# Two graph-attention layers on one core: where the store of the output stands in SyncE's order

## The chip, the core and the metric

The kernel runs on one core of a Trainium2 chip. A core has TensorE (PE in the profile, with its weight loads as PEld), VectorE (DVE), ScalarE (ACT), GpSimd (POOL) and SyncE (SP), which here does nothing but issue transfers. The metric is the time of one execution on the device in microseconds; lower is better.

## What is computed

The input is a batch of 64 graphs of 256 nodes with 512 features each, and an adjacency matrix for each graph. Two layers follow one another, each of the form x = x + layer(relu(layernorm(x))):

```python
# layer 0: two GAT sublayers, mask = adj or the diagonal, softmax over the sources
h = elu(gat_layer(h, mask, W1, att_src1, att_dst1, b1, concat=True))   # 4 heads of 256
h = gat_layer(h, mask, W2, att_src2, att_dst2, b2, concat=False)       # 1 head of 512
# layer 1: one sublayer, 8 heads of 64, mask = adj, softmax over the targets, relu
scores = leaky_relu(a_src[i] + a_dst[j] + b_att);  out = relu(softmax(scores) @ xh)
```

The graphs don't depend on each other.

## The kernel before

Each graph goes through three attention sublayers, numbered 1, 2 and 3 in the names of the steps. A sublayer is a product with the weights (`m1a` and `m1b`, `m2`, `m3`, each a set of seven smaller products, L54), the exponentials of the attention terms (`exp1`, `exp2`, `exp3`), the weights of the edges (`edges`, L280 on ScalarE and L281 on VectorE), a product with these (`gat1` L382, `gat2` L434, `gat3` L484), and a step that divides and adds on VectorE (`out1` L392, `out2` L444, `out3` L492). 128 nodes stand across the partitions, so a graph has two row tiles (T = 2).

**How a term gets to all partitions.** The edges need a term of every node along the free axis, alike on every partition. `spread` (L230) does it by way of DRAM: ScalarE issues a small write of the exponentials (`kept<-exs`, L233; 8 KB in `exp3`, 1 KB in `exp2`, 4 KB in `exp1`), and SyncE issues the reads that hand it to all 128 partitions (`bc<-kept`, L238; four of 256 KB in `exp3`, one of 128 KB in `exp2`, two of 256 KB in `exp1`). A read has to wait until the write has landed. L280 on ScalarE waits for the read.

**How the layernormed input is turned.** `away1` writes h to DRAM and reads it back in another layout (L200, L201); VectorE then transposes it (`back`, L206) for the products of `m1a` and `m1b`.

**The order.** There is no scheduler at work (`manual_schedule`): every engine runs its instructions in the order in which the program states them. A string named `order` is that order; it is gone through once for each round r from 1 to 63, with a `head` before and a `tail` after. An item such as `-2 store` is a step of graph r - 2, so that three or four graphs are under way in a round: graph r + 1 is loaded, normalised and multiplied by W1, graph r goes through sublayer 1 and into sublayer 2, graph r - 1 from sublayer 2 into 3, and graph r - 2 finishes sublayer 3. An item places its instructions on every engine that it uses, behind those of the items ahead of it; the place of `store`, which is one transfer on SyncE, matters on SyncE alone.

**SyncE in a round**, before: `cap3` (two transposing transfers, L363), `load` (xs and ad, L292 and L294), `away1` (L200, L201), the four reads of `exp3`, the read of `exp2`, the store of graph r - 2 (L501), the two reads of `exp1`. An instruction that waits holds up those behind it.

**The store.** `store` writes the tile x2 of graph r - 2, 512 KB, to the output. x2 is completed by four additions on GpSimd, two rows of tiles by two halves (`out3`, L494), the last of which is `-2 out3 1 0`. The pool of x2 has two buffers; `out2` of a later graph writes into the one that the store has freed.

Each transfer tells of its landing on one of eight semaphores that are given out in turn. [...]

Of the kernel before, what the change touches and what calls it, by code (L numbers as in the profile page):

```python
# [97 lines left out]
def short_path(ctx, tc, flags, x, adj, w1, att_src1, att_dst1, b1, w2, att_src2, att_dst2, b2, w_proj, w_att,  # L98
# [451 lines left out]
    class Weights:  # L550
# [66 lines left out]
        -2 edges3 7, -2 gat3 0 0, -2 edges3 5, -2 gat3 0 1, -1 edges2, 0 m1b p7, -2 out3 0 1, -2 out3 0 0,  # L617
        -1 gat2 0, 0 m1b c22, -1 out2 0, -1 stats3 0, 0 m1b p3, -1 gat2 1, 0 edges1 0, 0 edges1 1, 0 m1b p4,
        -1 out2 1, 0 cap3, 1 load, 0 gat1 0 0, 0 edges1 2, 0 edges1 3, 0 out1 0 0, -2 gat3 1 1, -2 gat3 1 0,
        -1 stats3 1, 0 gat1 0 1, -1 norm3, -2 out3 1 1, -2 out3 1 0, 0 out1 0 1, 0 elu1 0 0, 0 elu1 0 1, 0  # L620
        gat1 1 0, -1 turn3, 0 out1 1 0, 0 gat1 1 1, 0 out1 1 1, 1 stats1, -1 m3 p1, 0 turn2 0 0, 0 turn2 0
        1, 0 elu1 1 1, 0 elu1 1 0, -1 m3 p2, -1 m3 p5, 1 masks, 1 norm1, -1 m3 p6, 0 m2 p1, 0 turn2 1 0, 0
        turn2 1 1, 1 away1, -1 m3 p7, 1 bias, -1 m3 c22, 0 m2 p2, -1 m3 p4, -2 range, -1 m3 p3, -1 exp3, 1
        turn1, 0 m2 p6, 0 m2 p5, 0 m2 p7, 1 caps, 1 m1a p1, 0 m2 c22, 0 m2 p3, 0 m2 p4, 0 exp2, 1 m1a p6, -2
        store, -1 edges3 0, -1 edges3 1, 1 m1b p1, 1 m1a p7, 1 m1a p5, 1 m1a c22, -1 edges3 2, 1 m1a p2, -1
        edges3 4, 1 m1a p3, -1 edges3 3, 1 m1a p4, 1 m1b p2, 1 exp1, -1 edges3 6, 1 m1b p6, 1 m1b p5
    """
    tail = """
# [270 lines left out]
@with_exitstack  # L899
def gat_layers(ctx, tc, *args):  # L900
    nc = tc.nc
    pool = ctx.enter_context(tc.tile_pool(name="flags", bufs=1))
    flags = pool.tile([1, 1], I32, name="flags")
    short_path(tc, flags, *args)
    B = args[0].shape[0]
    count = nc.values_load(flags[0:1, 0:1], min_val=0, max_val=B)
    general_path(tc, count, *args)
# [24 lines left out]
```

## Time and profile before

| what | before |
|---|---|
| time, median of 3 runs | 3341.45 us (3340.55 to 3341.65) |
| span of the profiled execution | 3279.7 us |
| mean granted TensorE clock | 0.993 |
| TensorE busy | 3155.8 us, 96% |
| VectorE busy | 2267.6 us, 69% |
| ScalarE busy | 1959.6 us, 60% |
| GpSimd busy | 1178.3 us, 36% |
| transfers | 279.19 MB, 85 GB/s on average |

The busy times are those of an engine's own instructions; the issue of a transfer is not counted. The span of the profile runs from the first to the last instruction; the time of a run contains some 62 us more.

Three kinds of lines are used below. A line of the timeline has the start in us, the length in us, the engine (with a q where only its sequencer is at work), the line of the kernel, the operation, the tiles as out<-in, how many instructions are merged, and in brackets how long the engine stood idle before it and what ended that. A line of the waits says who waited for what, the total in us, how often, and the longest. A line of the table of stretches has the stretch, its length, for PE, PEld, DVE, ACT and POOL the busy time and the number of instructions, then the granted clock, the busy share of the 16 DMA engines and what they moved in GB/s. `kept<-exs`, `bc<-kept` and `out_dram<-x` are the small write, the read over all partitions and the store.

### The profile page before, as it was taken

How to read it: one execution, taken by the hardware profiler on the slowest of the kernel's cores; microseconds unless marked ns; L12 is line 12 of the kernel's file. 1: busy time of each engine (PE TensorE's matmuls, PEld its weight loads, DVE VectorE, ACT ScalarE, POOL GpSimd, SP SyncE). 2: the span in 40 equal slices, each digit the busy share in tenths (PEclk: the TensorE clock that was granted, in tenths of full speed). 3: DMA queues.
4: the chain of work that ended last, by engine and by line, in shares of the span. 5: the costliest groups of instructions: out<-in, count | busy, mean ns of one | idle time of the engine just before them, and what ended most of it. 6: DMA issues, size and time to landing. Idle time of an engine off the chain costs nothing. (4 is left out here: it accounts for less than half of the span.)

```text
span 3279.7 us, 60652 instructions
## 1 busy us (share of the span) xinstructions
PE 3155.8 (96%) x21808; PEld 2663.1 (81%) x21808; DVE 2267.6 (69%) x6189; ACT 1959.6 (60%) x4867; POOL 1178.3 (36%) x1433
## 2 busy tenths in 40 slices
PE   4999999999999999999999999999999999999997
PEld 3788888888888888888888888888888888888886
DVE  7667667667667677676676676676776766766765
ACT  2566566566556566655665565566566556665654
POOL 3243343343343342332433433423333334334332
PEclk8999999999999999999999999999999999999998
DMA  4222333323323333323223223233333233332231
GB/s 140 65 79 83 88 87 85 88 88 78 94 82 84 88 82 91 86 83 89 80 82 91 87 79 88 82 91 86 83 91 86 82 89 81 78 94 87 79 94 34
DMA packets 350751, 279.19 MB, mean 85 GB/s; under 512 B 157936, under 2 KB 252016, under 8 KB 350448
## 3 DMA queue, kind: packets, MB, share of 16 engines
q1 hardware_dynamic: 240688, 272.31, 28.3%
q10 hardware_dynamic: 109760, 2.95, 1.9%
q8 instruction: 177, 2.90, 0.4%
q14 instruction: 126, 1.03, 0.2%
HBM read 199.36 MB, written 67.43 MB: 81 GB/s over the span
## 5 line engine op out<-in xcount | busy, mean ns | idle before, releaser
L280 ACT ACTIVATE wy<-bc,exs 128x256 f32<-128x256 f32 x1646 | 746.9, 524 | 263.8 <-DMA bc<-kept 199.4
L281 DVE SCALAR_TENSOR_TENSOR e<-wy,exs,cap 128x256 f32<-128x256 f32 x1024 | 452.2, 483 | 223.0 <-ACT wy L280 223.0
L382 PE MATMUL pm<-xl,e 128*128 128x257 f32 x2048 | 500.3, 387 | 57.5 <-DVE e L281 21.7
L253 DVE TENSOR_TENSOR xl<-pm,kept 128x256 f32<-128x256 f32 (+2 forms) x768 | 321.8, 419 | 282.7 <-PE pm L54 196.9
L494 POOL TENSOR_TENSOR x<-x,o 128x256 f32<-128x256 f32 x256 | 181.0, 728 | 930.9 <-DVE r L490 884.2
L54 PE MATMUL sum<-w_sb,h1s 128*128 128x257 f32 x2048 | 489.0, 381 | 9.3 <-POOL h1s L213 7.0
L382 PEld LDWEIGHTS pm<-xl,e 128*128 128x128 f32 x2048 | 365.5, 190 | 151.4 <-DVE e L281 36.5
L60 ACT ACTIVATE kept<-sum 128x264 f32<-128x264 f32 (+3 forms) x768 | 276.7, 376 | 310.7 <-PE sum L54 294.3
L54 PEld LDWEIGHTS sum<-w_sb,h1s 128*128 128x128 f32 x2048 | 389.4, 190 | 68.7 <-POOL h1s L213 7.2
L54 PE MATMUL pm<-w_sb,h1s 128*128 128x257 f32 x1536 | 370.7, 383 | 10.4 <-DVE xl L253 7.1
L178 POOL TENSOR_TENSOR rstd<-ve,neg_half 128x2 f32<-128x2 f32 x128 | 117.6, 919 | 683.5 <-DVE ve L176 683.5
L54 PEld LDWEIGHTS pm<-w_sb,h1s 128*128 128x128 f32 x1536 | 286.7, 190 | 74.7 <-POOL hs L213 20.7
L281 DVE SCALAR_TENSOR_TENSOR e<-wy,exs,mask 128x256 f32<-128x256 f32 x640 | 276.0, 482 | 65.9 <-ACT wy L280 65.6
L484 PEld LDWEIGHTS pm<-xl,e 128*64 128x64 f32 x8192 | 251.8, 138 | 45.2 <-DVE e L281 23.3
L54 PE MATMUL sum<-w1a_sb,hs 128*128 128x260 f32 x1024 | 269.8, 386 | 11.7 <-DVE w1a_sb L520 4.1
L54 PE MATMUL sum<-w1b_sb,hs 128*128 128x256 f32 x1024 | 271.7, 388 | 4.1 <-ACT hs L343 1.9
L484 PE MATMUL pm<-xl,e 128*64 128x65 f32 x8192 | 270.4, 224 | 1.9 <-DVE e L281 1.2
L54 PE MATMUL sum<-wp_sb,hs 128*128 128x264 f32 x1024 | 271.0, 387 | 1.1 <-ACT kept L60 1.1
L395 ACT ACTIVATE ez<-z 128x512 f32<-128x512 f32 x256 | 159.8, 624 | 181.6 <-DVE z L392 181.6
L392 DVE SCALAR_TENSOR_TENSOR z<-pm,r,b_sb 128x256 f32<-128x256 f32 x512 | 247.8, 484 | 18.3
L434 PE MATMUL pm<-xl,e 128*128 128x257 f32 (+1 forms) x1024 | 243.8, 381 | 1.2 <-DVE e L281 1.2
L54 PEld LDWEIGHTS sum<-w1a_sb,hs 128*128 128x128 f32 x1024 | 190.7, 190 | 51.1 <-issue 13.2
(97 smaller groups left out, 4962.9 us busy)
## 6 DMA issues: line engine op xcount, KB each, us to landing
bc<-kept SPq DMA_DIRECT2D x380, 256.0 KB
xs<-in_x_dram SPq DMA_DIRECT2D x64, 512.0 KB
out_dram<-x SPq DMA_DIRECT2D x64, 512.0 KB
kept_h<-h SPq DMA_DIRECT2D x63, 512.0 KB
h<-kept_h SPq DMA_DIRECT2D x63, 512.0 KB
ad<-in_adj_dram SPq DMA_DIRECT2D x64, 256.0 KB
bc<-kept SPq DMA_DIRECT2D x63, 128.0 KB
w_sb<-in_L_gnn_W_dram SPq DMA_DIRECT2D x4, 512.0 KB
```

The source lines that it names most:

```text
L54: self.nc.tensor.matmul(to[:, :self.n], self.lhs[:, i, c, :], self.rhs[:, i, c, :], start=(first and c == 0), stop=(last and c == self.nk ...
L60: self.nc.scalar.activation(s[:, :self.n], self.sum[:, :self.n], AF.Copy)
L178: nc.gpsimd.tensor_tensor(rstd, ve[:, 0, :], neg_half, ALU.pow)
L253: nc.vector.tensor_tensor(dst, pm, add, ALU.add)
L280: nc.scalar.activation(wy, bc, AF.Copy, scale=yw)
L281: nc.vector.scalar_tensor_tensor(dst, wy.rearrange("p t q -> p (t q)"), xw, mask, ALU.max, op)
L382: nc.tensor.matmul(pm[:, :Q + 1], self.e[1, h][:, s, t * P:(t + 1) * P], xl1[:, s, h, L1:], start=(s == 0), stop=(s == T - 1))
L392: nc.vector.scalar_tensor_tensor(z[:, sl], pm[:, :Q], r, b1_sb[:, sl], ALU.mult, ALU.add)
L395: nc.scalar.activation(ez, z[:, 2 * g * F1:2 * (g + 1) * F1], AF.Relu, scale=-1.0)
L434: nc.tensor.matmul(pm[:, :n], self.e[2][:, s, t * P:(t + 1) * P], xl2[:, s, half, L2:L2 + n], start=(s == 0), stop=(s == T - 1))
L484: nc.tensor.matmul(pv[q:q + 64, h, :], self.e[3, a * G + h][:, s, t * P + q:t * P + q + 64], xl3[:, s, a * G + h, :], start=(s == 0), stop ...
L494: nc.gpsimd.tensor_tensor(to, to, o.rearrange("p h k -> p (h k)"), ALU.add)
```

## The change

The item `-2 store` goes from the end of the round, behind `1 m1a p6`, to right behind `-2 out3 1 0`, the last addition to its tile. It is meant to send the output off as soon as it is complete. In SyncE's order the store then stands behind `load` and ahead of `away1`; everything else keeps its order. The head and the tail, which has the last two stores, are as before.

```diff
-        -1 stats3 1, 0 gat1 0 1, -1 norm3, -2 out3 1 1, -2 out3 1 0, 0 out1 0 1, 0 elu1 0 0, 0 elu1 0 1, 0
+        -1 stats3 1, 0 gat1 0 1, -1 norm3, -2 out3 1 1, -2 out3 1 0, -2 store, 0 out1 0 1, 0 elu1 0 0, 0
...
-        turn1, 0 m2 p6, 0 m2 p5, 0 m2 p7, 1 caps, 1 m1a p1, 0 m2 c22, 0 m2 p3, 0 m2 p4, 0 exp2, 1 m1a p6, -2
-        store, -1 edges3 0, -1 edges3 1, 1 m1b p1, 1 m1a p7, 1 m1a p5, 1 m1a c22, -1 edges3 2, 1 m1a p2, -1
+        m1a p6, -1 edges3 0, -1 edges3 1, 1 m1b p1, 1 m1a p7, 1 m1a p5, 1 m1a c22, -1 edges3 2, 1 m1a p2, -1
```

The lines between are the same items, broken at other places.

More of the change, by code (lines that the diff above doesn't have):

```diff
@@ L619, in short_path @@
         -1 out2 1, 0 cap3, 1 load, 0 gat1 0 0, 0 edges1 2, 0 edges1 3, 0 out1 0 0, -2 gat3 1 1, -2 gat3 1 0,
-        -1 stats3 1, 0 gat1 0 1, -1 norm3, -2 out3 1 1, -2 out3 1 0, 0 out1 0 1, 0 elu1 0 0, 0 elu1 0 1, 0
-        gat1 1 0, -1 turn3, 0 out1 1 0, 0 gat1 1 1, 0 out1 1 1, 1 stats1, -1 m3 p1, 0 turn2 0 0, 0 turn2 0
-        1, 0 elu1 1 1, 0 elu1 1 0, -1 m3 p2, -1 m3 p5, 1 masks, 1 norm1, -1 m3 p6, 0 m2 p1, 0 turn2 1 0, 0
-        turn2 1 1, 1 away1, -1 m3 p7, 1 bias, -1 m3 c22, 0 m2 p2, -1 m3 p4, -2 range, -1 m3 p3, -1 exp3, 1
-        turn1, 0 m2 p6, 0 m2 p5, 0 m2 p7, 1 caps, 1 m1a p1, 0 m2 c22, 0 m2 p3, 0 m2 p4, 0 exp2, 1 m1a p6, -2
-        store, -1 edges3 0, -1 edges3 1, 1 m1b p1, 1 m1a p7, 1 m1a p5, 1 m1a c22, -1 edges3 2, 1 m1a p2, -1
+        -1 stats3 1, 0 gat1 0 1, -1 norm3, -2 out3 1 1, -2 out3 1 0, -2 store, 0 out1 0 1, 0 elu1 0 0, 0
+        elu1 0 1, 0 gat1 1 0, -1 turn3, 0 out1 1 0, 0 gat1 1 1, 0 out1 1 1, 1 stats1, -1 m3 p1, 0 turn2 0 0,
+        0 turn2 0 1, 0 elu1 1 1, 0 elu1 1 0, -1 m3 p2, -1 m3 p5, 1 masks, 1 norm1, -1 m3 p6, 0 m2 p1, 0
+        turn2 1 0, 0 turn2 1 1, 1 away1, -1 m3 p7, 1 bias, -1 m3 c22, 0 m2 p2, -1 m3 p4, -2 range, -1 m3 p3,
+        -1 exp3, 1 turn1, 0 m2 p6, 0 m2 p5, 0 m2 p7, 1 caps, 1 m1a p1, 0 m2 c22, 0 m2 p3, 0 m2 p4, 0 exp2, 1
+        m1a p6, -1 edges3 0, -1 edges3 1, 1 m1b p1, 1 m1a p7, 1 m1a p5, 1 m1a c22, -1 edges3 2, 1 m1a p2, -1
         edges3 4, 1 m1a p3, -1 edges3 3, 1 m1a p4, 1 m1b p2, 1 exp1, -1 edges3 6, 1 m1b p6, 1 m1b p5
```

## Prediction

> **What bounds the kernel now.** I read the page first, for the engine that is nearly full and how little of it is idle.
>
> ```profile
> span 3279.7 us, 60652 instructions
> PE 3155.8 (96%) x21808; PEld 2663.1 (81%) x21808; DVE 2267.6 (69%) x6189; ACT 1959.6 (60%) x4867; POOL 1178.3 (36%) x1433
> ```
>
> TensorE (PE) is the bound; a change that only moves a store can win no more than TensorE's idle time. The table of stretches says where that is. I cut the span at the first L434 matmul (`gat2`) of each round. The rows are one round without the store, three with it, and the 59 rounds from 201.25 to 3143.63 together; the second number is the round's length, the third TensorE's busy time.
>
> ```profile
> 152.44:201.25 48.81, 48.60 (x341) 41.49 (x340) 34.71 (x94) 30.62 (x76) 18.18 (x22) 1.00 0.32 88
> 1596.30:1647.17 50.87, 48.92 (x341) 41.24 (x340) 34.66 (x95) 30.53 (x76) 18.17 (x22) 1.00 0.30 84
> 1494.98:1545.98 51.00, 48.91 (x341) 41.27 (x340) 34.70 (x95) 30.55 (x76) 18.16 (x22) 1.00 0.34 83
> 2446.26:2494.91 48.65, 48.50 (x341) 41.49 (x340) 34.70 (x95) 30.52 (x76) 18.19 (x22) 1.00 0.29 87
> 201.25:3143.63 2942.38, 2882.47 (x20061) 2438.95 (x20060) 2048.34 (x5546) 1802.18 (x4484) 1072.12 (x1298) 1.00 0.31 86
> ```
>
> The same work takes 48.65 to 51.00 us at a clock of 1.00 throughout; the mean is 2942.38 / 59 = 49.87. So a round that waits for nothing takes about 48.7, and 1.2 us a round is lost. Third view, the waits of TensorE from 110 to 3160 us (total, times, longest):
>
> ```profile
> PE pm L382 <- DVE r L390: 21.1, 48, 0.6
> PE pm L382 <- DVE r L490: 13.2, 52, 0.3
> PE pm L382 <- DVE e L281: 12.1, 21, 1.2
> PE pm L54 <- DVE xl L253: 6.1, 40, 0.2
> ```
>
> 46 us of it stand before L382, `gat1`, in the first microseconds of a round: VectorE is late with `edges1` (L281), then with `out1` and `out3`, which stand behind them on VectorE. Why it is late shows in the timeline of one such round, ScalarE, SyncE and TensorE in turn:
>
> ```profile
> 1589.08 0.39 SPq L501 DMA_DIRECT2D out_dram<-x  x1
> 1591.35 0.37 ACTq L233 DMA_DIRECT2D kept<-exs  x1
> 1598.31 0.79 SPq L238 DMA_DIRECT2D bc<-kept  x2
> 1601.62 1.77 ACT L280 ACTIVATE wy<-bc,exs 128x256 f32<-128x256 f32 x4 [4.73 <-DMA bc<-kept]
> 1602.71 2.00 PE L382 MATMUL pm<-xl,e 128*128 128x257 f32 x8 [1.06 <-DVE e L281]
> ```
>
> and in the one full round that has no store to make (round 1: graph -1 doesn't exist):
>
> ```profile
> 147.49 0.37 ACTq L233 DMA_DIRECT2D kept<-exs  x1
> 150.63 0.79 SPq L238 DMA_DIRECT2D bc<-kept  x2
> 157.63 1.90 PE L382 MATMUL pm<-xl,e 128*128 128x257 f32 x8
> ```
>
> The chain is `exp1`'s 4 KB write of exs to DRAM (L233), its read back over all partitions (L238, issued only once the write has landed), then L280, L281, L382. From write to read it takes 1598.31 - 1591.35 = 6.96 us with the store issued 2.3 us ahead of the write, and 3.14 without; and there TensorE waits for nothing. I took these points in every round: with the store 4.2 to 7.0, median 5.7 (61 rounds); the three writes without it (two in the head, one in round 1) took 3.03, 4.62 and 3.14.
>
> **What the Trainium skill says.** "DMA: Bandwidth & Descriptors", section "Queues, rings and completion order": SyncE's and ScalarE's queues are rings on the same 16 engines, served in turn, and the write that raises a transfer's semaphore lands only after all earlier writes of that engine, across its queues. So the small write must wait out the store's writes even where its own bytes are through. The trace agrees: the last 8-byte packet of the write leaves a median 2.6 us after issue with the store and 1.7 in round 1, and from there the read follows after 3.1 and 1.4 us. Same page, "Latency and other measured facts": the receipt from HBM grows with load; here the whole write to read grows from 3.14 to 5.7.
> "Perfetto Trace Analysis", "Per-instruction lifecycle": a DMA's bar is its issue, not its movement. So I read movement from the DMA share of stretches, here 2 us each, then the stretch in which the store will stand:
>
> ```profile
> 147.50:149.50 2.00, 2.00 (x12) 1.49 (x10) 1.67 (x5) 1.80 (x7) 0.00 (x0) 1.00 0.64 61
> 1591.00:1593.00 2.00, 2.00 (x11) 1.75 (x10) 1.80 (x5) 1.80 (x8) 0.00 (x0) 1.00 0.97 242
> 1662.00:1671.00 9.00, 9.00 (x52) 7.86 (x51) 7.43 (x22) 7.15 (x13) 4.17 (x6) 1.00 0.00 0
> ```
>
> While the write goes out, the engines are 97% busy at 242 GB/s with the store, and 64% at 61 GB/s without.
>
> **The change, part by part.**
> *What moves.* No instruction is added or removed; 62 of the 64 stores (rounds 2 to 63) go up SyncE's order, from behind bc2's read to behind `load` and ahead of `away1`. On the other engines only names and the numbers of DMA semaphores shift.
> *What is taken away.* The store from ahead of `exp1`'s write. Then the read of bc1 is issued 1.1 us (5.7 to 4.6) to 2.6 us (5.7 to 3.1) earlier. What a round gains I take from the 59 rounds: with d the time from the L434 anchor to bc1's issue (mean +0.65 us), the length follows 48.75 + 0.97 x max(0, d + 0.50) us; by groups, d under -0.2 gives 48.73 (6 rounds), 0.2 to 0.7 gives 49.63 (13), over 1.3 gives 50.70 (8). So all of the lateness is paid, down to d = -0.5. Moving every d earlier by 1.0, 1.5 and 2.5 us gives mean lengths of 49.09, 48.85 and 48.75: 46, 60 and 66 us over 59 rounds. I take 1.5, between the ends, because three writes are few and an instruction fetch crosses them at times: 60 us. The tail's first round, with a late bc1 too (4.29 us of wait on ScalarE), may add 1; I leave it out.
> *What the store meets at its new place.* It waits for GpSimd's last addition. In the round at 1647 that ends at 1660.39 + 1.42 = 1661.81. Behind it on SyncE stands `away1`'s write, which waits for ScalarE's `norm1` until 1671.17: the store waits on 5 us in which SyncE would have waited anyway, and 9.4 us remain for 512 KB. Where it stands now its packets take 2.6 us (from 0.6 before the small write's issue to 2.0 after); with about 1 us to the first packet and 3 to the landing, an estimate from the small write's own 3.14, it is over by 1668. The DMA engines carry nothing from 1662 to 1671, and no tile for `turn2`, `m3` or `stats1` is in transfer then: cost nothing.
> *Buffers.* x2 (two buffers) comes free some 29 us sooner (1691.08 to about 1662); VectorE waited for that 0.3 us once in the whole run. Nothing.
> *Sum.* 3341.45 - 60 = 3281.
>
> **The rivals.**
> *Less of it:* the small write is slow for another reason as well. bc2's read, just ahead of it, and instruction fetches stay; the write in the head without a store took 4.62. A gain of only 0.5 us in d gives 49.44 a round: 26 us, 3316. Against it: the longest wait for bc1 and the store's last packet go together (0.82 between the last packets of store and write).
> *No change:* once bc1 comes in time, L382 waits for `out1` or `out3` through VectorE's own queue, so that the reciprocals' 34 us stay: 3341.45 - 12 at most for L281 alone, and with an unlucky rest 3338. Against it: round 1, and the fast rounds such as 2446.26, have none of these waits at equal VectorE work (34.7 us).
> *Slower:* the store collides with `away1`: write and read back of h (1671.17, 1674.42), which VectorE's L206 awaited in 58 rounds, 46 us in all, so the path has no slack. If it ran on 1 us into it, 62 x 1 would be lost against the 60 won; if 1.5 and half the gain comes, 3341 + 93 - 30 = 3404. Against it: the 9.4 us.
>
> **How the numbers follow.** Most of the gain, 3281: 0.67. Less of it, 3316: 0.20. No change: 0.06. Slower: 0.07. The lower end of the range is all lateness gone, 66 us and a little from head and tail: 3270. The upper end takes in the partial case: 3318. Faster by over 0.2% (below 3334.8) is the first two: 0.87; the same 0.06; slower 0.07.
>
> **What would show it.** In the profile after: from L233's 4 KB write to bc1's read about 3.1 to 4.2 us instead of 5.7; rounds of 48.7 to 48.9 us; TensorE's waits before L382 down from 46 us to under 10; the store issued some 13 to 14 us after the L434 anchor, and the DMA share between 1662 and 1671 of such a round no longer 0. TensorE's busy time stays near 3150. I am wrong if that write still takes over 5 us, if L382 still waits for VectorE in most rounds, or if L206's wait for h grows above its 46 us.

## The result, and the profile after

The changed kernel takes 3228.09 us (median of 4 runs, 3224.51 to 3231.37), against 3341.55 us before (3340.55 to 3341.86). The ratio is 0.9661, with a 95% interval of 0.9644 to 0.9677: faster by 113 us. The forecast was 3281 us with a range of 3270 to 3318, so the direction was right and the gain almost twice as large.

The head of the page after, to be read against the two lines of before:

```profile
span 3227.2 us, 60529 instructions
PE 3146.1 (97%) x21808; PEld 2670.1 (83%) x21808; DVE 2266.0 (70%) x6189; ACT 1963.0 (61%) x4867; POOL 1178.1 (37%) x1433
```

The busy times are nearly the same; the span is 52.5 us shorter. This is the first thing to notice: between the two traces lie 52.5 us, between the timed runs 113. The table of stretches, for the same 59 rounds and for one of them:

```profile
204.78:3092.43 2887.65, 2870.73 (x20062) 2444.60 (x20061) 2046.90 (x5547) 1805.56 (x4484) 1072.01 (x1298) 1.00 0.33 87
1624.82:1673.49 48.67, 48.52 (x341) 41.49 (x340) 34.73 (x95) 30.66 (x76) 18.19 (x22) 1.00 0.31 87
```

The mean round is 2887.65 / 59 = 48.94 us (median 48.81), where it was 49.87. TensorE's waits from 110 to 3100 us:

```profile
PE pm L54 <- DVE xl L253: 4.8, 32, 0.2
PE pm L382 <- DVE r L490: 2.3, 10, 0.3
PE pm L382 <- DVE r L390: 2.2, 6, 0.6
PE pm L434 <- DVE e L281: 2.0, 2, 1.2
PE sum L54 <- ACT kept L60: 1.9, 7, 0.4
PE pt L193 <- ACT h L186: 1.8, 2, 1.5
PE pm L382 <- DVE e L281: 1.4, 2, 0.7
```

What stood before L382 was 46.4 us (12.1 for L281, 34.3 for the two reciprocals); it is 5.9. Of the 54.7 us that the 59 rounds are shorter, that is some 40; another 11.7 is TensorE's busy time, 2870.73 instead of 2882.47 for the same matmuls, which the profile doesn't explain. The timeline of one round, ScalarE, SyncE and TensorE:

```profile
1619.87 0.37 ACTq L233 DMA_DIRECT2D kept<-exs  x1
1623.55 0.79 SPq L238 DMA_DIRECT2D bc<-kept  x2
1627.55 1.90 ACT L280 ACTIVATE wy<-bc,exs 128x256 f32<-128x256 f32 x4 [2.15 <-DMA bc<-kept]
1630.01 1.90 PE L382 MATMUL pm<-xl,e 128*128 128x257 f32 x8
1637.46 0.38 SPq L501 DMA_DIRECT2D out_dram<-x  x1
1646.80 0.37 SPq L200 DMA_DIRECT2D kept_h<-h  x1
```

From exp1's small write to the read of bc1 it takes 3.68 us here instead of 6.96, and L382 starts with no wait. The store is issued 12.6 us after the first L434 (at 1624.82) and 9.3 us ahead of `away1`. VectorE's wait for what `away1` reads back is about what it was (46.0 us before):

```profile
DVE hs L206 <- DMA h<-kept_h: 47.2, 56, 2.1
```

### The profile page after: what moved, and what is told of

Read it like the earlier page. It is cut to its first block, busy times and chain, and to the rows that moved or that the text cites. A ratio compares the mean times of both kernels' runs of the same rounds, so it can differ in the third digit from the quotient of the medians.

```text
span 3227.2 us, 60529 instructions
## 1 busy us (share of the span) xinstructions
PE 3146.1 (97%) x21808; PEld 2670.1 (83%) x21808; DVE 2266.0 (70%) x6189; ACT 1963.0 (61%) x4867; POOL 1178.1 (37%) x1433
## 5 line engine op out<-in xcount | busy, mean ns | idle before, releaser
L280 ACT ACTIVATE wy<-bc,exs 128x256 f32<-128x256 f32 x1646 | 745.4, 524 | 187.5 <-DMA bc<-kept 141.7
L281 DVE SCALAR_TENSOR_TENSOR e<-wy,exs,cap 128x256 f32<-128x256 f32 x1024 | 452.0, 483 | 223.4 <-ACT wy L280 223.3
L382 PE MATMUL pm<-xl,e 128*128 128x257 f32 x2048 | 495.6, 387 | 15.1 <-DVE e L281 10.2
L54 PE MATMUL sum<-w_sb,h1s 128*128 128x257 f32 x2048 | 489.1, 381 | 9.3 <-POOL h1s L213 7.0
L382 PEld LDWEIGHTS pm<-xl,e 128*128 128x128 f32 x2048 | 374.0, 190 | 87.6 <-issue 14.1
L54 PEld LDWEIGHTS sum<-w_sb,h1s 128*128 128x128 f32 x2048 | 389.4, 190 | 68.7 <-POOL h1s L213 7.2
L54 PE MATMUL pm<-w_sb,h1s 128*128 128x257 f32 x1536 | 371.2, 383 | 10.4 <-DVE xl L253 5.9
L54 PEld LDWEIGHTS pm<-w_sb,h1s 128*128 128x128 f32 x1536 | 287.0, 190 | 74.8 <-POOL hs L213 17.0
L281 DVE SCALAR_TENSOR_TENSOR e<-wy,exs,mask 128x256 f32<-128x256 f32 x640 | 276.1, 482 | 15.6 <-ACT wy L280 15.3
L54 PE MATMUL sum<-w1a_sb,hs 128*128 128x260 f32 x1024 | 270.2, 387 | 7.9 <-ACT kept L60 2.9
L54 PE MATMUL sum<-w1b_sb,hs 128*128 128x256 f32 x1024 | 272.6, 389 | 4.2 <-DVE w1b_sb L520 2.2
L54 PE MATMUL sum<-wp_sb,hs 128*128 128x264 f32 x1024 | 271.0, 387 | 1.1 <-ACT kept L60 1.1
L434 PE MATMUL pm<-xl,e 128*128 128x257 f32 (+1 forms) x1024 | 245.6, 382 | 3.5 <-DVE e L281 3.4
L54 PEld LDWEIGHTS sum<-w1a_sb,hs 128*128 128x128 f32 x1024 | 190.7, 190 | 47.7 <-issue 13.4
```

What stands on the lines that cost most here:

```text
L54: self.nc.tensor.matmul(to[:, :self.n], self.lhs[:, i, c, :], self.rhs[:, i, c, :], start=(first and c == 0), stop=(last and c == self.nk ...
L280: nc.scalar.activation(wy, bc, AF.Copy, scale=yw)
L281: nc.vector.scalar_tensor_tensor(dst, wy.rearrange("p t q -> p (t q)"), xw, mask, ALU.max, op)
L382: nc.tensor.matmul(pm[:, :Q + 1], self.e[1, h][:, s, t * P:(t + 1) * P], xl1[:, s, h, L1:], start=(s == 0), stop=(s == T - 1))
L434: nc.tensor.matmul(pm[:, :n], self.e[2][:, s, t * P:(t + 1) * P], xl2[:, s, half, L2:L2 + n], start=(s == 0), stop=(s == T - 1))
```

## The experiments

Three quantities recur. *d* is the time from the first L434 of a round to the issue of bc1's read, *write to read* that from exp1's small write to that read, both averaged over 59 rounds of a run's trace. *Formula* is the prediction's 48.75 + 0.97 x max(0, d + 0.50), taken round by round and averaged; it was fitted on the first trace of before alone.

```
run            chip  timed us   write to read    d     round   formula
before (1st)    -    (traced 3281) 5.61        0.65   49.87   49.87
b_again         5     3381.8       7.11        2.16   51.51   51.33
e_load          5     3357.8       6.20        1.19   50.95   50.40
e_hop           5     3376.1       7.00        1.96   51.23   51.14
after           -     3228.1       4.06       -0.93   48.94   48.82
after_again    11     3219.9       3.91       -1.04   48.86   48.79
e_without      11     3221.1       3.96       -1.00   48.92   48.81
e_half         11     3243.0       4.70       -0.25   49.21   49.18
e_behind       11     3463.4       3.91       -1.05   52.78   48.79
a_ctrl          1     3229.6       4.07       -0.90   48.92   48.82
e_first         1     3240.2       5.09       -0.81   49.14   49.03
b_first         1     3339.6       7.40        1.58   50.76   50.77
```

The experiments fell on three chips; on these before took 3382.8 (chip 5), 3309.7 (chip 11) and 3342.6 (chip 1). The chips of before (1st) and after are not on record. The ratios below are against before on the same chip.

**The kernel before, unchanged (b_again).** No edit.

> The kernel before, unchanged, once more, for its trace. Of the 113 us gained, 55 are in the trace of before (59 rounds of 49.87 against 48.94); the other 58 are that before took 3341 us in its timed runs and 3281 in the traced one. Theory: the traced execution was a luckier one, the small write of exp1 competing with the store in a varying way; if this trace is of an execution near 3341, its rounds are about 50.9 us and bc1's read is issued about 1.6 us after the L434 anchor in nearly all of them (write to read about 6.5 us instead of a median 5.7). Rival 1: the trace itself or the chip makes the difference, then this trace again has 49.9 us rounds while the timed runs say 3341. Rival 2: the 58 us are lost elsewhere in the round, then the trace of a 3341 us execution shows write to read near 5.7 and another wait of TensorE. Ratio 1.000 in any case.

Timed 3381.84, ratio 0.999 (0.9977 to 1.0003), and the traced execution has a span of 3378.7: trace and timed runs agree here. The stretch of 59 rounds and the waits of TensorE from 110 to 3250 us:

```profile
202.47:3241.43 3038.96, 2901.59 (x20061) 2443.59 (x20060) 2046.25 (x5546) 1803.23 (x4484) 1073.85 (x1298) 1.00 0.31 83
```

```profile
PE pm L382 <- DVE e L281: 87.3, 60, 2.3
PE pm L382 <- DVE r L390: 25.2, 52, 0.6
PE pm L382 <- DVE r L490: 13.0, 51, 0.3
```

The additional time stands before the same instruction, L382, now in nearly every round: 125.5 us in place of 46.4. Write to read went from 5.61 to 7.11 and d from 0.65 to 2.16; the formula gives 51.33 a round of the 51.51 found. So the kernel before is one whose loss depends on how long its small write takes, and the first trace had caught an execution where that was short. Here the trace shows what the timed runs do, and TensorE's waits grow at L382 and nowhere else: both rivals fall for this execution. The one at 3341 us itself was not traced. A spread of 60 us isn't seen within a set of runs: the four at 3341 us lie within 1.3 us of each other, the 27 of before on this chip within 25 us, and in every other row of the table the traced execution is one of the timed ones. Whether the first trace of before was taken on another chip than its timed runs is not on record.

**Lateness without a store (e_hop).**

```diff
-    def spread(w, heads):
+    def spread(w, heads, hop=False):
...
+        if hop:
+            first, kept = kept, dram.tile([heads, P, T], F32, name="again")
+            nc.sync.dma_start(kept, first)
...
-            self.bc1 = spread(self.ex1[:, 2 * H1:], H1)
+            self.bc1 = spread(self.ex1[:, 2 * H1:], H1, self.b > 1)
```

> The store at its new place, and exp1's 4 KB copied once more within DRAM before it is read, in rounds of graphs 2 and later: bc1 comes late without any store near it. Theory (lateness of bc1 alone sets the round): a copy that has to land costs about 3 us, d goes from -0.9 to about +2.1, rounds are 48.75 + 0.97 x 2.6 = 51.3 us and the time is 3228 + 61 x 2.4 = 3374, range 3340 to 3400, ratio 1.00 to 1.018; traced and timed executions agree within 10 us. Rival (bc1's lateness is only a part, the store's traffic also slows something else): 3260 to 3310, ratio 0.975 to 0.99.

3376.14, ratio 0.998 (0.9968 to 0.9992): the store is at its new place, and all the gain but 7 us is gone. d is 1.96, the formula gives 51.14, the trace has 51.23. TensorE's waits from 110 to 3160 us stand before the same matmul again (lines are three further down in this kernel, so that L385, L284, L393 and L493 are L382, L281, L390 and L490):

```profile
PE pm L385 <- DVE e L284: 68.3, 54, 2.8
PE pm L385 <- DVE r L393: 26.7, 55, 0.6
PE pm L385 <- DVE r L493: 13.8, 54, 0.3
```

The lateness of bc1 alone makes the round long; the store is one way to cause it.

**The changed kernel twice more, on chips 11 and 1 (after_again, a_ctrl).** No edit.

> The changed kernel once more, on the chip of these runs. The second trace of before (3379 us) had d = 2.16 us on average and rounds of 51.51, where 48.75 + 0.97 x (2.16 + 0.50) gives 51.33; so the step that mis-sized the gain was d itself, which differs from chip to chip and execution to execution with the store in the way. Theory: the changed kernel's time hardly depends on the chip, since d stays under -0.5 in most rounds (the copy run had 4.4 us from exp1's write to the first read without a store near, d = -0.55): 3225 to 3245 us, and the ratio to a before near 3382 is 0.954 to 0.960. Rival (the chip of these runs is slower in other ways too): 3265 us or more, ratio 0.965 to 0.97.

> The changed kernel a third time, beside the two that follow. It has been 3228 and 3220 where before was 3342 and 3310; before has been 3310 to 3383. Theory: 3215 to 3240 whatever before takes here.

The chip of after_again was another than expected, one on which before takes 3309.71: 3219.90, ratio 0.9727 (0.971 to 0.9743). The time is 5 us under the range that I gave, and the ratio, which took before to be at 3382, missed. a_ctrl: 3229.55 against 3342.57, ratio 0.9669 (0.9652 to 0.9687). So the changed kernel has been 3220 to 3230 in three sets, and before 3310 to 3383 in four: in these sets, what makes the gain differ is the kernel before. The changed kernel was not run on chip 5, where before is slowest.

**No store at all (e_without).** It leaves the 62 stores of the rounds out, so most of the output is not written.

```diff
-... 1 m1a p6, -2
-        store, -1 edges3 0, ...
+... 1 m1a p6,
+        -1 edges3 0, ...
```

> Leaves out the 62 stores of the rounds, so most of the output is not written. Theory (the store cost time only by delaying exp1's small write, and its new place costs nothing): within 10 us of the changed kernel on the same chip. Rival (the new place costs something too): 15 us or more below it.

3221.11 beside after_again's 3219.90: the store at its new place costs nothing that can be measured.

**Half of the store at each place (e_half).** `-2 early` stores the first row tile at the new place, `-2 late` the second at the old one.

```diff
+        def part(self, a, n):
+            nc.sync.dma_start(out[self.b].rearrange("(t p) d -> p t d", p=P)[:, a:n], self.x2[:, a:n])
...
-        ... -2 out3 1 0, -2 store, ...
+        ... -2 out3 1 0, -2 early, ...
...
-        m1a p6, -1 edges3 0, ...
+        m1a p6, -2 late, -1 edges3 0, ...
```

> Half of the store (256 KB, the first row tile) at its new place, half where it stood before. Theory (the small write waits for the store's packets to pass, so lateness goes with the bytes): write to read about half way between the two kernels, d half way too; since the round is flat below d = -0.5, 45 to 60 percent of the gain remains: with before near 3382 a time of 3285 to 3325, ratio 0.971 to 0.983. Rival (any write to HBM ahead makes the semaphore wait for a receipt, whatever its size): nearly all of the loss stays, ratio over 0.99.

3242.98, ratio 0.9797 (0.9781 to 0.9813): 66.7 of the 89.8 us that after_again gains, 74%, more than the 45 to 60% expected. Write to read is 4.70, where the changed kernel has 3.91 on this chip (before was not traced on it); d = -0.25 gives 49.18 by the formula, and 49.21 is found. The lateness grows with the bytes ahead; the rival falls.

**A load in the store's place (e_load).** `ghost` reads 512 KB into the tile that has been stored.

```diff
+        def ghost(self):
+            nc.sync.dma_start(self.x2, x[self.b].rearrange("(t p) d -> p t d", p=P))
...
-        m1a p6, -1 edges3 0, ...
+        m1a p6, -2 ghost, -1 edges3 0, ...
```

> The store at its new place, and where it stood a load of the same size (512 KB from HBM into the x2 tile that has just been stored, whose content is used no more). Theory as the prediction had it (the small write's semaphore has to wait for the store's writes to HBM): a load writes nothing to HBM, so most of the gain stays: write to read under 4.8 us, 3228 to 3265, ratio 0.966 to 0.977. Rival (it is the occupancy of the 16 DMA engines alone, 512 KB in about 2.6 us): write to read 5.5 us or more, 3290 to 3341, ratio 0.985 to 1.00.

3357.76, ratio 0.9915 (0.9891 to 0.994), write to read 6.20: a load costs most of what the store cost, as the rival said, and my expectation was wrong. The transfer records of the three runs of chip 5 split write to read (means in us; e_hop up to its first copy, with neither store nor load ahead):

```
                  first packet   last packet   landed and read issued, after the last packet
e_hop, neither        0.95          1.84            2.57
e_load, load          1.99          3.64            2.56
b_again, store        1.62          3.54            3.56
```

Store and load alike hold the small write's packets up by 1.7 to 1.8 us. Only the store also makes the landing 1.0 us longer. So of the 2.7 us that the store costs, some two thirds are its packets on the 16 engines and one third comes with its being a write to HBM. Of e_load's 0.55 us over the formula an estimated 0.2 are the clock (see below); bc1's own read also took some 0.4 us longer from issue to L280 than in e_hop (3.94 against 3.50 on average). That these two are all of it is not shown; VectorE also waited 6.4 us in all for the load before L444.

**The store one step later (e_behind).** `-2 store` stands behind `1 exp1`, so that in SyncE's order it follows bc1's reads.

> The store neither at its old place nor right behind the last addition, but at the round's end, one step further on than before: behind exp1's two reads instead of ahead of them. Theory (what counts is that it doesn't stand ahead of exp1's write in the queues, not that it is early): write to read as in the changed kernel, about 4.2 us, and within 10 us of it; a few us more at most where the store still moves when bc1's second half does or when cap's transposes and xs follow. Rival (being early is what helps, by freeing x2 or by leaving the queue to the reads): the store now shares the engines with bc1's reads, bc1 lands 1 us or more later, and 40 us or more are lost against the changed kernel.

3463.44, ratio 1.0469 (1.0448 to 1.0491): 154 us slower than before. Write to read is 3.91, exactly as in the changed kernel; that half of the theory holds. What I had overlooked is in the waits, of all engines and then of TensorE:

```profile
DVE x L444 <- DMA out_dram<-x: 242.6, 61, 5.4
```

```profile
PE pm L434 <- DVE x L444: 142.7, 59, 4.1
PE pm L382 <- DVE r L390: 12.7, 29, 0.6
PE pm L382 <- DVE r L490: 7.4, 29, 0.3
```

`out2` (L444) writes into the x2 tile that this store still reads; it now waits 4 us in every round, and the second half of `gat2` (L434) for it. In before that wait was 0.3 us in all, in b_again 30.8. So the place has two bounds: just ahead of exp1's write it holds that write up, and behind bc1's reads it is too late for the two buffers. A third x2 buffer, which would separate the two, was not tried.

**The write a little earlier (e_first on the changed kernel, b_first on before).**

```diff
-        edges3 4, 1 m1a p3, -1 edges3 3, 1 m1a p4, 1 m1b p2, 1 exp1, -1 edges3 6,
+        edges3 4, 1 m1a p4, 1 exp1, -1 edges3 3, 1 m1a p3, 1 m1b p2, -1 edges3 6,
```

> The changed kernel with m1a's p4 ahead of p3 on TensorE and exp1 right behind it: exp1's write leaves one group of four matmuls (0.87 us) earlier. Theory: d, about -1.0 on average with a tail above -0.5 in a quarter of the rounds, goes to about -1.9, and nearly all rounds run at 48.65 to 48.7: 5 to 15 us less than the changed kernel. Rival (the rest of 0.2 to 0.3 us a round over 48.65 has nothing to do with bc1): within 4 us of it; or slower by 10 us and more, if p3 being later makes TensorE wait for the bank that its sum leaves.

> The same edit on the kernel before, the store where it stood. Theory (a round is late by what bc1 is late, whatever makes it so): d falls by 0.87 us less what the small write loses by leaving closer behind the store (2.0 instead of 2.8 us after its issue, so up to all of it): 0 to 50 us less than before on the same chip, middle 25, ratio 0.985 to 1.0. It stays clear of the changed kernel by 50 us or more. Rival (the order of exp1's write against the store doesn't matter, the order of p3 and p4 does): as fast as the changed kernel.

The write does leave some 0.9 us earlier (5.90 us ahead of the first L434 in e_first, 4.97 in a_ctrl), and nothing comes of it. b_first: 3339.60, ratio 0.9998 (0.9986 to 1.0011), at the edge of what I expected. e_first: 3240.24 against a_ctrl's 3229.55, 11 us slower, so my expectation was wrong in sign. In e_first write to read rises from 4.07 to 5.09: the write now meets the last of bc2's 128 KB read, and its last packet leaves 2.4 us after issue instead of 1.6. The rival, that the later p3 makes TensorE wait, forecast the 11 us but isn't what the trace shows: TensorE's waits for VectorE before L54 are 5.3 us against a_ctrl's 6.1, those before L382 11.4 against 4.3, and the formula gives 0.21 of the 0.22 us a round. Here the traffic ahead of the write took back what its earlier issue won. None of these variants is faster than the changed kernel.

## Why the prediction was wrong

- **The chain** (small write, read, L280, L281, L382, and TensorE's 46 us before L382): right. These waits are 5.9 us after, and e_hop makes them with no store near.
- **The gain as d changes:** right in form and size. d moved by 1.58 us (0.65 to -0.93) where I took 1.5, a value picked between 1.1 and 2.6, so that its closeness is partly luck; write to read is 4.06 where I gave 3.1 to 4.2. The two traces differ by 52.5 us where I had 60. The formula holds within 0.2 us a round in nine of the ten other runs in which bc1 sets the round, e_load being the exception.
- **The step that failed is the starting value of d, and with it the loss per round: the 60 in "3341.45 - 60 = 3281", which measured 113.** I wrote "the mean is 2942.38 / 59 = 49.87", "1.2 us a round is lost", and took 60 us off 3341.45. But 49.87 belongs to the traced execution, which as a run took 3281.43 us; the runs that gave 3341.45 were another 60 us longer, and I had booked that difference as time outside the span (the "some 62 us more" ahead of the prediction). It isn't: a run is only 1.7 us longer than its span (3281.43 to 3279.7, and 3228.96 to 3227.2 after). The timed runs' rounds were thus about (3341.5 - 1.7 - 337.3) / 59 = 50.9 us, with 337.3 us of head and tail from the trace; by the formula d was 1.7. From 50.9 to 48.94 over 59 rounds is 115 us, less 2.3 us of longer head and tail: 113. This divides the measured difference up and is no check of it. That d was 1.7 in those runs is worked out, not traced; two traces make it likely: b_again, the same kernel, with d = 2.16 at a span of 3379 us, and b_first, with the store at its old place, timed at 3340, with d = 1.58 and rounds of 50.76.
- **The lower end of the range failed with it:** "66 us and a little" for all lateness gone is the traced execution's bound; the timed one's, worked out the same way, was (50.9 - 48.75) x 59 = 127.
- **The new place costs nothing:** right. e_without is as fast; L206's wait for h is 47.2 us, where it was 46.0; the store waits on GpSimd for 374.6 us in 64 cases, 5.9 us on average, time in which SyncE would have waited for `norm1` (its wait before L200 fell from 933.9 to 594.2 us).
- **Buffers:** right for this change, but "nothing" hid that x2 was close to binding; e_behind and b_again (30.8 us) show it.
- **The Trainium skill's ordering of completions** ("DMA: Bandwidth & Descriptors", section "Queues, rings and completion order") can account for the smaller part alone: 1.0 us of 2.7. Whether the landing waits for the store's writes, as that section has it, or is itself slower while HBM is being written, no run separates. The larger part fits what the same section says of queues that are served in turn on the same 16 engines: e_load shows the small write's packets held up by 1.8 us.
- **The rivals:** none came about.

What makes the small write slower on one chip than on another with the same traffic ahead (5.61, 7.11 and, from the timed runs, values between) stays open. Of the 1.5 us between the two traces, 0.9 come before the write's last packet (2.65 and 3.53 us after issue) and 0.6 behind it. The store stands somewhat closer ahead of the write in b_again (2.3 us against 2.8 on average), but where it stands 2.2 to 2.6 us ahead in both, write to read still takes 5.8 and 7.15 us. With nothing big ahead it differs much less: 3.91 to 4.4 us over the traces of after, after_again, a_ctrl and e_hop (up to its copy).

## What to carry to other kernels

Where a small write has to land before others can read it back, look at what is issued just ahead of it, on another engine's queue too: half a megabyte on SyncE's cost ScalarE's write 2.7 us in each round (b_again against e_hop), on a path that TensorE waited for, while the DMA engines were idle for 9 us at a stretch elsewhere in the round. Moving the store to that gap was free (e_without), since nothing needed its buffer sooner; on the same chip, one place too late cost 154 us against the place before, and the new place won 90. And before a trace's loss is taken as the loss of the timed runs, compare the traced execution's own time with theirs: here they differed by 60 us, and a run is only 1.7 us longer than its span, so the loss per round differed too.

## What the runs showed of the hardware

- Transfers that contend are where this kernel's time varies: with the store ahead of the small write the four medians of before spread over 73 us (3310 to 3383); with it away, three medians lie within 10 us. Only the set on chip 5, the slowest for before, has no run of the changed kernel beside it.
- Waits of TensorE of 2 us and more went together with spells at half its clock. In e_behind the granted clock was 0.977 on average, with 29 spells at half speed between 200 and 3100 us, of 3.4 to 6.8 us each, 109 us in all; before and after have none there. Each of the 29 began within a wait of 1.9 to 4.1 us or at most 1.3 us behind its end; of the 51 waits over 1.9 us in that stretch, 22 brought none on. In b_again 7 of 14 such waits did, in e_load 6 of 8, in e_hop 5 of 11; of the 71 waits of 1.0 to 1.9 us in these four runs none did (e_without has one spell behind a wait of 1.5 us). One such, in the table of stretches (TensorE waits 2.76 us up to 1692.3; the third number from the end is the clock):

```profile
1686.00:1690.00 4.00, 3.57 (x17) 2.79 (x15) 1.25 (x5) 1.13 (x3) 1.41 (x2) 1.00 0.71 234
1690.00:1694.00 4.00, 1.67 (x5) 1.45 (x6) 2.23 (x6) 0.59 (x2) 0.00 (x0) 0.86 0.32 62
1694.00:1698.00 4.00, 4.00 (x24) 3.04 (x24) 3.95 (x11) 2.58 (x6) 0.00 (x0) 0.71 0.20 12
1698.00:1702.00 4.00, 4.00 (x71) 3.66 (x68) 3.75 (x15) 1.79 (x3) 1.47 (x3) 1.00 0.52 191
```

  If half of each spell is lost, an estimate, the 109 us are some 55 us of e_behind's loss. b_again's 7 spells (24 us) would be 12 us lost, about the 0.2 us a round by which it exceeds the formula; e_load's 6 come to 24 us too.
